# A pairwise outer product with batch normalization: long rows in descending order, stored in longer runs

## The chip, the cores and the metric

The kernel runs on one core of a Trainium2 chip. The time is that of one execution on the device, in microseconds (us); with one core it is that core's time. The profile is of one execution: its span runs from the first instruction to the last, and is a little shorter than the time of the execution.

## The reference

There are 1024 samples, 39 fields and 16 values a field. For each of the 741 pairs of fields (row r from 1 to 38, column c below r) the outer product of `xj[r]` and `xi[c]` is taken, normalized over all samples and its 256 entries, scaled and shifted by the pair's `gamma` and `beta`, and multiplied by `W`:

```python
_ROWS, _COLS = np.tril_indices(39, k=-1)          # 741 pairs, row by row
cross = xj[:, rows, :, None] * xi[:, cols, None, :]         # (1024, 741, 16, 16)
mean = jnp.mean(cross, axis=(0, 2, 3), keepdims=True)
var = jnp.mean(jnp.square(cross - mean), axis=(0, 2, 3), keepdims=True)
normed = (cross - mean) * jax.lax.rsqrt(var + 1e-5)
normed = normed * gamma[None, :, None, None] + beta[None, :, None, None]
out = normed[:, :, None, :, :] * W[None, None, :, :, :]
return jnp.transpose(out, (0, 2, 1, 3, 4))        # (1024, 1, 741, 16, 16) float32
```

The output is 777 MB; a pair of one sample is 256 values, 1 KB. In memory a sample's pairs lie one behind the other, row 1 first, so a row of r pairs is r KB without a gap, once for each sample.

## The kernel before

**Statistics.** Both inputs are loaded whole (6 MB). Each partition holds eight samples (`NT = 8`). Mean and variance of all pairs come from sums and a few small matrix products, without forming the pairs. From them `spread(group)` puts the scale and shift of some rows on all partitions (matrix products into PSUM), and `apply(group)` (L493 to L500, DVE) folds `gamma` and `beta` in and leaves the two coefficients of each pair in `st_sb`. `ROW_GROUPS` lists the groups: first row, last row plus one, PSUM bank, and the tile `n` behind which the group is applied. `SHORT_GROUP` names the group of rows 1 to 4.

**Tiles.** A tile is one row for two samples per partition (`T = 2`, 256 samples in all, so four tiles per row). The list `tiles` holds the row, the first of its two samples (`t0`), and its place in `y_sb`, counted in pairs. It begins with row 19 four times (tiles 0 to 3). Then come rows 20 to 38 in ascending order, each tile of a row r followed by a tile of its partner row 38 - r (row 38 has none). A row and its partner fill one half of `y_sb` (`half` = 76 pairs x 1 KB per partition), and the halves are used in turn. In its place a tile holds the r pairs of its first sample, then those of its second, and behind both stands the partner. Tiles 0 and 1 lie in the first half, 2 and 3 in the second; the statistics use the second half as scratch before.

**The steps of a tile.** The coefficients are folded in as follows:
- `scale_xi(n)` (L167, POOL) multiplies `xi` by the scale of each pair and leaves it in `xs` (two buffers).
- `products(n)` writes the outer products into `y_sb`: for each sample and each of the 16 values of `xj[r]` one instruction over all r pairs, some on ACT (L145), some on POOL (L147). POOL takes 4 of 16, or 5 for rows over 33 (`LONG`), or 6, 6, 5 for tiles 0 to 2. Rows 1 to 4 (`SHORT`) are done by DVE instead (L180, L190), from `xj_short`, a copy in PSUM that ACT makes once (L526).
- `finish(n)` adds the shift and multiplies by `W` in place. DVE does it by one L284 for a pair, both samples at once (tile 1, `RAW`, has one sample at a time). Some pairs are taken off DVE: POOL adds the shift (L270) and multiplies a few pairs together (L273); for rows over 33, ACT adds it (L268) and POOL multiplies, eight pairs in two steps of four.
- `store(n, c0, c1, t_from, t_to)` (L209) puts the pairs c0 to c1 out as DMAs of SP's queue. `bounds(n)` cuts a tile into pieces: by hand for the first eight (`FIRST_PIECES`), then one piece up to row `ONE`, two above. A store goes out when its piece is finished. The last piece of a row over `ONE` is one DMA for each sample; every other piece is one DMA for both.

Tile 0 takes another path (`affine` and `weigh`), which starts from raw products made during the statistics.

**Order.** The order on each engine is that of the program (`manual_schedule`), and engines wait for each other where data or places overlap. The loop over n issues `scale_xi(n + 2)`, `finish(n)`, `apply` of the groups due, and `products(n + 1)`. So on ACT the L268 of a tile stand ahead of the products of the next, on POOL stand `xs`, the end of the tile, then the next products, and on SP all stores stand in the order of the tiles. Products of a tile may start when the stores of what lay in its place have landed.

Of the kernel before, what the change touches and what calls it, by code (L numbers as in the profile page):

```python
# [14 lines left out]
T = 2  # L15


ONE, LONG = 24, 33
FIRST_PIECES = (
    (0, 1, 3, 6, 10, 14, 19), (0, 4, 9, 14, 19), (0, 4, 11, 19), (0, 9, 19), (0, 10, 20), (0, 9, 18), (0, 10, 20), (0, 9, 18)  # L20
)


# [6 lines left out]


ROW_GROUPS = (
    (19, 20, 0, None), (20, 21, 1, None), (15, 19, 1, 2), (21, 25, 2, 4), (1, 15, 2, 8), (25, 32, 3, 16), (32, 39, 4, 24)
)
SHORT_GROUP = 4


@with_exitstack
def tile_pair_outer_batchnorm(
# [17 lines left out]
    NB, F, E = xi.shape  # L57
# [8 lines left out]
    mid = (F - 1) // 2  # L66
    tiles = [(mid, t0, t0 // T * half // 2) for t0 in range(0, NT, T)]
    slot = 0
    for r in range(mid + 1, F):
        for t0 in range(0, NT, T):  # L70
            tiles.append((r, t0, slot * half))
            if r < F - 1:
                tiles.append((F - 1 - r, t0, slot * half + T * r))
            slot ^= 1

    RAW = 1
# [58 lines left out]
    def view(n):  # L135
        r, _, u = tiles[n]
        return y_sb[:, u : u + T * r, :].rearrange("p (t n) e -> p t n e", t=T)
# [23 lines left out]
    def scale_xi(n):  # L161
        r, t0, _ = tiles[n]
        if r <= SHORT:
            return
        n0 = first[r]
        xs = scaled.tile([P, T, r, E], F32, tag="xs", name=f"xs_{r}_{t0}")
        nc.gpsimd.tensor_tensor(  # L167
            xs,
            xi_sb[:, t0 : t0 + T, 0:r, :],
            s_sb[:, :, n0 : n0 + r, :].to_broadcast([P, T, r, E]),  # L170
            ALU.mult,
        )
        xs_of[n] = xs

    def products(n):

        r, t0, _ = tiles[n]
        if r <= SHORT:
            xs = scaled_short.tile([P, T, r, E], F32, tag="xs_short", name=f"xs_{r}_{t0}")
            nc.vector.tensor_tensor(  # L180
                xs,
                xi_sb[:, t0 : t0 + T, 0:r, :],
                s_short[:, first[r] : first[r] + r]
                .unsqueeze(1)
                .unsqueeze(3)
                .to_broadcast([P, T, r, E]),
                ALU.mult,
            )
            for t in range(T):
                nc.vector.tensor_tensor(  # L190
                    view(n)[:, t].rearrange("p n (i j) -> p n i j", j=E),
                    xs[:, t].unsqueeze(2).to_broadcast([P, r, E, E]),
                    xj_short[:, t0 + t, r - 1 : r, :].unsqueeze(3).to_broadcast([P, r, E, E]),
                    ALU.mult,
                )
            return
        xs = xs_of.pop(n)
        split = E - (POOL_I_FIRST[n] if n < 3 else POOL_I_LONG if tiles[n][0] > LONG else POOL_I)
        for t in range(T):
            for i in range(E):  # L200
                product(n, nc.scalar if i < split else nc.gpsimd, t, i, xs[:, t])

    def store(n, c0, c1, t_from=0, t_to=T):
        r, t0, _ = tiles[n]
        n0 = first[r]

        step = 1 if r > ONE and c1 == r else t_to - t_from
        for t in range(t_from, t_to, step):
            nc.sync.dma_start(  # L209
                out_v[:, t0 + t : t0 + t + step, (n0 + c0) * EE : (n0 + c1) * EE],  # L210
                view(n)[:, t : t + step, c0:c1, :].rearrange("p t n e -> p t (n e)"),
            )
# [14 lines left out]
    def weigh(n):  # L227

        y = view(n)
        for c0, c1 in zip(bounds(n), bounds(n)[1:]):  # L230
            affine(n, range(c0, min(c1, OWN)), (nc.vector,))
            nc.vector.tensor_tensor(  # L232
                y[:, :, c0:c1, :],
                y[:, :, c0:c1, :],
                w_dve.unsqueeze(1).to_broadcast([P, T, c1 - c0, EE]),
                ALU.mult,
            )
            store(n, c0, c1)

    def bounds(n):  # L240
        if n < len(FIRST_PIECES):
            return FIRST_PIECES[n]
        r = tiles[n][0]
        pieces = 1 + (r > ONE)
        return tuple(q * r // pieces for q in range(pieces + 1))

    def finish(n):


        r = tiles[n][0]  # L250
        n0 = first[r]
        y = view(n)
        long = r > LONG
        p1 = r // 2 if long else r
        if long:
            share = POOL_PAIRS_LONG
        elif RAW < n < 10:
            share = POOL_PAIRS_FIRST
        else:
            share = int(r * POOL_SHARE + 0.5) if r > SHORT else 0  # L260
        p0 = p1 - share
        step = POOL_PAIRS_LONG // 2 if long else r
        for c0 in range(p0, p1, step):
            c1 = min(c0 + step, p1)
            for c in range(c0, c1):
                t_c = t_sb[:, n0 + c : n0 + c + 1]
                if long:
                    nc.scalar.activation(y[:, :, c, :], y[:, :, c, :], AF.Identity, bias=t_c)  # L268
                else:
                    nc.gpsimd.tensor_scalar(  # L270
                        y[:, :, c, :], y[:, :, c, :], t_c, 1.0, ALU.add, ALU.mult
                    )
            nc.gpsimd.tensor_tensor(  # L273
                y[:, :, c0:c1, :],
                y[:, :, c0:c1, :],
                w_sb.unsqueeze(1).to_broadcast([P, T, c1 - c0, EE]),
                ALU.mult,
            )

        size = 1 if n == RAW else T  # L280
        for t in range(0, T, size):
            for c0, c1 in zip(bounds(n), bounds(n)[1:]):
                for c in [*range(c0, min(c1, p0)), *range(max(c0, p1), c1)]:
                    stt(  # L284
                        y[:, t : t + size, c, :],
                        y[:, t : t + size, c, :],
                        t_sb[:, n0 + c : n0 + c + 1],
                        w_dve.to_broadcast([P, size, EE]),
                        ALU.add,
                        ALU.mult,  # L290
                    )
                store(n, c0, c1, t, t + size)

    with tc.manual_schedule():
# [180 lines left out]
        def spread(group):  # L475
            r0, r1, bank, _ = ROW_GROUPS[group]
            n0, n1 = first[r0], first[r1 - 1] + r1 - 1
            at = used[bank]
            used[bank] = at + 2 * (n1 - n0)
            ps = ps_st[bank][:, at : used[bank]].rearrange("p (x n) -> p x n", x=2)  # L480
            for r in range(r0, r1):
                nc.tensor.matmul(  # L482
                    ps[:, :, first[r] - n0 : first[r] - n0 + r],
                    pick[:, r, :],
                    stq[:, :, 0:r],
                    start=True,
                    stop=True,
                )
            spread_of.append((ps, n0, n1))

        def apply(group):
            ps, n0, n1 = spread_of[group]
            nc.vector.tensor_mul(ps[:, 1], ps[:, 1], st_sb[:, 0, n0:n1])  # L493
            if group == SHORT_GROUP:

                nc.vector.tensor_mul(ps[:, 0], ps[:, 0], st_sb[:, 0, n0:n1])
                nc.vector.tensor_copy(st_sb[:, 0, n0:n1], ps[:, 0])
            else:
                nc.vector.tensor_mul(st_sb[:, 0, n0:n1], ps[:, 0], st_sb[:, 0, n0:n1])
            nc.vector.tensor_add(st_sb[:, 1, n0:n1], ps[:, 1], st_sb[:, 1, n0:n1])  # L500
# [8 lines left out]
        for group in range(1, len(ROW_GROUPS)):  # L509
            spread(group)  # L510
        s_short = spread_of[SHORT_GROUP][0][:, 0]
        apply(1)
        products(1)
        scale_xi(2)

        for n in range(1, len(tiles)):
            if n + 2 < len(tiles):
                scale_xi(n + 2)
            finish(n)
            for group, (_, _, _, tile_of) in enumerate(ROW_GROUPS):  # L520
                if n == tile_of:
                    apply(group)
            if n + 1 < len(tiles):
                products(n + 1)
            if n == 32:
                nc.scalar.copy(xj_short, xj_sb[:, :, 1 : SHORT + 1, :])  # L526


# [26 lines left out]
```

## Time and profile before

| what | value |
|---|---|
| median of six runs | 1881.4 us (1880.85 to 1882.86) |
| the profiled execution | 1881.56 us, span 1879.8 us |
| DVE busy | 1720.5 us, 92% of the span |
| ACT busy | 1642.9 us, 87% |
| POOL busy | 1532.1 us, 82% |
| written to memory | 776.99 MB, 417 GB/s over the span |
| DMA packets | 63994 |
| first store issued | 36.03 us |
| last store issued | 1861.92 us |

Busy time of an engine counts its instructions alone. A DMA packet is one run that one of the 16 DMA engines moves; 128 partitions are spread over them, eight to an engine. Of the packets, 4784 have under 512 bytes, most of them the writes of 4 bytes by which a DMA tells that it has landed. The rest of the profile is shown where it is used.

### The profile page before, as it was taken

How to read it: one execution, taken by the hardware profiler on the slowest of the kernel's cores; microseconds unless marked ns; L12 is line 12 of the kernel's file. 1: busy time of each engine (PE TensorE's matmuls, PEld its weight loads, DVE VectorE, ACT ScalarE, POOL GpSimd, SP SyncE). 2: the span in 40 equal slices, each digit the busy share in tenths (PEclk: the TensorE clock that was granted, in tenths of full speed). 3: DMA queues.
4: the chain of work that ended last, by engine and by line, in shares of the span. 5: the costliest groups of instructions: out<-in, count | busy, mean ns of one | idle time of the engine just before them, and what ended most of it. 6: DMA issues, size and time to landing. Idle time of an engine off the chain costs nothing. (4 is left out here: it accounts for less than half of the span.)

```text
span 1879.8 us, 9660 instructions
## 1 busy us (share of the span) xinstructions
PE 26.0 (1%) x130; PEld 23.3 (1%) x130; DVE 1720.5 (92%) x2625; ACT 1642.9 (87%) x3416; POOL 1532.1 (82%) x1746
## 2 busy tenths in 40 slices
PE   4000000000000000000000000000000000000000
PEld 4000000000000000000000000000000000000000
DVE  8999999998989898989898989898999999988885
ACT  7998989898989798989898989898988888888883
POOL 8999888888888788888888878787888777777873
DMA  5999999999999999999999999999999999999999
GB/s 198 386 421 426 430 426 430 426 426 425 425 427 424 424 424 426 424 426 424 424 424 426 424 426 423 417 425 422 423 419 426 423 424 422 424 419 415 426 414 411
DMA packets 63994, 783.63 MB, mean 417 GB/s; under 512 B 4784, under 2 KB 6448, under 8 KB 17072
## 3 DMA queue, kind: packets, MB, share of 16 engines
q1 hardware_dynamic: 62624, 779.72, 98.3%
q10 hardware_dynamic: 1296, 3.29, 0.5%
q14 instruction: 73, 0.60, 0.1%
q8 instruction: 1, 0.02, 0.0%
HBM read 6.00 MB, written 776.99 MB: 417 GB/s over the span
## 5 line engine op out<-in xcount | busy, mean ns | idle before, releaser
L284 DVE SCALAR_TENSOR_TENSOR y_sb<-y_sb,st_sb,w_dve 128x512 f32<-128x512 f32 (+1 forms) x2511 | 1651.0, 737 | 132.2 <-issue 119.6
L145 ACT ACTIVATE y_sb<-xs,xj_sb 128x288 f32<-128x288 f32 (+20 forms) x3194 | 1510.8, 566 | 192.8 <-DMA out_dram<-y_sb 165.2
L147 POOL TENSOR_SCALAR y_sb<-xs,xj_sb 128x416 f32<-128x416 f32 (+29 forms) x1126 | 604.8, 561 | 40.9 <-DMA out_dram<-y_sb 27.7
L273 POOL TENSOR_TENSOR y_sb<-y_sb,w_sb 128x2048 f32<-128x2048 f32 (+3 forms) x155 | 517.3, 3343 | 104.0 <-ACT y_sb L268 94.5
L167 POOL TENSOR_TENSOR xs<-xi_sb,st_sb 128x640 f32<-128x640 f32 (+33 forms) x135 | 184.0, 1363 | 171.2 <-ACT y_sb L145 164.9
L270 POOL TENSOR_SCALAR y_sb<-y_sb,st_sb 128x512 f32<-128x512 f32 x291 | 196.8, 692 | 0.1
L268 ACT ACTIVATE y_sb<-y_sb,st_sb 128x512 f32<-128x512 f32 x160 | 100.2, 708 | 1.9
L190 DVE TENSOR_TENSOR y_sb<-xs,ps 128x1024 f32<-128x1024 f32 (+3 forms) x32 | 24.8, 817 | 0.6
L482 PE MATMUL ps<-y_sb 39*128 39x38 f32 (+37 forms) x76 | 16.5, 398 | 2.8 <-DVE y_sb L468 2.8
L482 PEld LDWEIGHTS ps<-y_sb 39*128 39x128 f32 x76 | 16.3, 329 | 3.1 <-DVE y_sb L468 3.1
L346 ACT ACTIVATE y_sb<-y_sb 128x1248 f32<-128x1248 f32 x8 | 9.9, 1244 | 2.8 <-POOL y_sb L335 2.7
L351 DVE TENSOR_REDUCE y_sb<-y_sb 128x78 f32<-128x1248 f32 x8 | 11.2, 1446 | 0.3 <-ACT y_sb L346 0.3
L145 ACT ACTIVATE y_sb<-xi_sb,xj_sb 128x304 f32<-128x304 f32 x24 | 11.4, 537 | 0.0
L335 POOL TENSOR_TENSOR y_sb<-xi_sb,y_sb 128x1248 f32<-128x1248 f32 x4 | 9.2, 2319 | 2.4 <-ACT y_sb L384 2.4
L232 DVE TENSOR_TENSOR y_sb<-y_sb,w_dve 128x2048 f32<-128x2048 f32 (+4 forms) x6 | 10.7, 1838 | 0.1
L325 DVE TENSOR_REDUCE y_sb<-xi_sb 128x39 f32<-128x624 f32 (+1 forms) x6 | 6.1, 1012 | 3.8 <-DMA xi_sb<-in_r_xi_dram 3.8
L335 POOL TENSOR_TENSOR y_sb<-xj_sb,y_sb 128x1248 f32<-128x1248 f32 x4 | 9.2, 2316 | 0.0
L371 PE MATMUL ps<-y_sb 128*39 128x79 f32 x48 | 8.1, 340 | 15.6 <-DVE y_sb L351 15.4
L225 POOL TENSOR_SCALAR y_sb<-y_sb,st_sb 128x512 f32<-128x512 f32 x8 | 6.4, 812 | 2.1 <-ACT y_sb L145 2.1
L325 DVE TENSOR_REDUCE y_sb<-xj_sb 128x39 f32<-128x624 f32 (+1 forms) x6 | 6.1, 1016 | 1.2 <-DMA xj_sb<-in_r_xj_dram 1.2
L223 ACT ACTIVATE y_sb<-y_sb,st_sb 128x512 f32<-128x512 f32 x9 | 6.5, 800 | 0.2 <-ACT y_sb L145 0.2
L371 PEld LDWEIGHTS ps<-y_sb 128*39 128x39 f32 x48 | 5.9, 178 | 17.6 <-DVE y_sb L351 10.4
(59 smaller groups left out, 35.1 us busy)
## 6 DMA issues: line engine op xcount, KB each, us to landing
out_dram<-y_sb SPq DMA_DIRECT2D x25, 2304.0 KB, 14.7
out_dram<-y_sb SPq DMA_DIRECT2D x12, 4352.0 KB, 15.4
out_dram<-y_sb SPq DMA_DIRECT2D x12, 4096.0 KB, 16.3
out_dram<-y_sb SPq DMA_DIRECT2D x10, 4608.0 KB, 14.7
out_dram<-y_sb SPq DMA_DIRECT2D x12, 3840.0 KB, 17.5
out_dram<-y_sb SPq DMA_DIRECT2D x21, 2048.0 KB, 17.0
out_dram<-y_sb SPq DMA_DIRECT2D x12, 3584.0 KB, 18.1
out_dram<-y_sb SPq DMA_DIRECT2D x12, 3328.0 KB, 18.1
```

Source lines behind the costliest of these rows:

```text
L145: nc.scalar.activation(y, src, AF.Copy, scale=scale)
L147: engine.tensor_scalar(y, src, scale, 1.0, ALU.mult, ALU.mult)
L167: nc.gpsimd.tensor_tensor(xs, xi_sb[:, t0 : t0 + T, 0:r, :], s_sb[:, :, n0 : n0 + r, :].to_broadcast([P, T, r, E]), ALU.mult,)
L190: nc.vector.tensor_tensor(view(n)[:, t].rearrange("p n (i j) -> p n i j", j=E), xs[:, t].unsqueeze(2).to_broadcast([P, r, E, E]), xj_short ...
L268: nc.scalar.activation(y[:, :, c, :], y[:, :, c, :], AF.Identity, bias=t_c)
L270: nc.gpsimd.tensor_scalar(y[:, :, c, :], y[:, :, c, :], t_c, 1.0, ALU.add, ALU.mult)
L273: nc.gpsimd.tensor_tensor(y[:, :, c0:c1, :], y[:, :, c0:c1, :], w_sb.unsqueeze(1).to_broadcast([P, T, c1 - c0, EE]), ALU.mult,)
L284: stt(y[:, t : t + size, c, :], y[:, t : t + size, c, :], t_sb[:, n0 + c : n0 + c + 1], w_dve.to_broadcast([P, size, EE]), ALU.add, ALU.mult,)
L325: nc.vector.tensor_reduce(total[:, t0:t1, part(x)], sources[x][:, t0:t1], AX.X, ALU.add)
L335: nc.gpsimd.tensor_tensor(devs[n % 7], sources[x][:, t0 : t0 + T], shift[:, x : x + 1, :].unsqueeze(3).to_broadcast([P, T, F, E]), ALU.sub ...
L371: nc.tensor.matmul(ps_g[acc][0:F, 0 : 2 * F + 1], lhs, fb[:, t], start=t == 0, stop=t == NT - 1)
L482: nc.tensor.matmul(ps[:, :, first[r] - n0 : first[r] - n0 + r], pick[:, r, :], stq[:, :, 0:r], start=True, stop=True,)
```

## The change

It has four parts. The rows over 19 come in descending order, 38 first; row 38 so fills the places of tiles 0 to 3, and row 20 comes last. `ONE` goes from 24 to 30, so rows 25 to 30 are one piece. From tile 6 on, `store` writes rows over 19 one sample at a time: the first sample in its pieces, the second sample whole, at the last piece. The first two tiles of row 38 (4 and 5) are cut into four pieces by hand, of which the last is one DMA for each sample. The groups of rows, the tile at which `xj_short` is copied and the tiles with `POOL_PAIRS_FIRST` follow the new order; the coefficients of the second group are applied in the loop at n = 1 and not ahead of `products(1)`.

```diff
-ONE, LONG = 24, 33
+ONE, LONG = 30, 33
 FIRST_PIECES = (
-    (0, 1, 3, 6, 10, 14, 19), (0, 4, 9, 14, 19), (0, 4, 11, 19), (0, 9, 19), (0, 10, 20), (0, 9, 18), (0, 10, 20), (0, 9, 18)
+    (0, 1, 3, 6, 10, 14, 19), (0, 4, 9, 14, 19), (0, 4, 11, 19), (0, 9, 19), (0, 10, 19, 29, 38), (0, 10, 19, 29, 38)
 )
 ROW_GROUPS = (
-    (19, 20, 0, None), (20, 21, 1, None), (15, 19, 1, 2), (21, 25, 2, 4), (1, 15, 2, 8), (25, 32, 3, 16), (32, 39, 4, 24)
+    (19, 20, 0, None), (38, 39, 1, 1), (34, 38, 1, 4), (1, 5, 1, 5), (29, 34, 2, 28), (5, 10, 2, 29),
+    (25, 29, 3, 68), (10, 14, 3, 69), (20, 25, 4, 100), (14, 19, 4, 101),
 )
-SHORT_GROUP = 4
+SHORT_GROUP = 3
...
-    for r in range(mid + 1, F):
+    for r in range(F - 1, mid, -1):
         for t0 in range(0, NT, T):
             tiles.append((r, t0, slot * half))
...
-        step = 1 if r > ONE and c1 == r else t_to - t_from
+        whole = n >= len(FIRST_PIECES)
+        step = 1 if r > mid and (whole or c1 == r) else t_to - t_from
         for t in range(t_from, t_to, step):
+            if whole and step == 1 and t == t_to - 1:
+                if c1 < r:
+                    continue
+                c0 = 0
             nc.sync.dma_start(
...
-        elif RAW < n < 10:
+        elif RAW < n < 4:
             share = POOL_PAIRS_FIRST
...
-        apply(1)
         products(1)
         scale_xi(2)
...
-            if n == 32:
+            if n == 5:
                 nc.scalar.copy(xj_short, xj_sb[:, :, 1 : SHORT + 1, :])
```

## The prediction

> **What bounds the kernel now.** I read the page's slices first, then the DMA view over long stretches, then the time line of single engines, and the chain of waits last.
>
> ```profile
> DVE  8999999998989898989898989898999999988885
> ACT  7998989898989798989898989898988888888883
> DMA  5999999999999999999999999999999999999999
> GB/s 198 386 421 426 430 426 430 426 426 425 425 427 424 424 424 426 424 426 424 424 424 426 424 426 423 417 425 422 423 419 426 423 424 422 424 419 415 426 414 411
> ...
> q1 hardware_dynamic: 62624, 779.72, 98.3%
> ```
>
> From the third slice on the 16 DMA engines are busy throughout; no compute engine is. The end is set by 777 MB going out. So only three things count: when the first store starts, what a byte costs, and the holes in which DMA has nothing to send. A store in flight hides every engine's work.
>
> What a packet costs comes from the DMA view of two stretches with one form of store each (rows 20 to 23, one run per sample; rows 25 to 30, two runs):
>
> ```profile
> DMA packets 5444, 100.02 MB, mean 427 GB/s; under 512 B 320, under 2 KB 320, under 8 KB 320
> ...
> DMA packets 19769, 237.79 MB, mean 425 GB/s; under 512 B 1516, under 2 KB 1516, under 8 KB 1772
> ```
>
> The first is 200 to 434 us, the second 600 to 1160 us. Packets under 512 B are 4-byte semaphore writes, so 5124 and 18253 carry data. Sixteen engines give 16 x 234 = 3744 = 5124a + 100.02b and 16 x 560 = 8960 = 18253a + 237.79b; hence a = 0.0097 us per packet and b = 36.94 engine-us per MB. Put into 83 to 1862 us (754.02 MB, 53286 data packets) this needs 28368 / 16 = 1773.0 of 1779 us: **6.0 us of holes**. 1390 to 1860 us (rows 34 to 38; 197.90 MB, 14496 packets) holds 4.3 of them.
>
> ```profile
> 424.76 7.43 ACT L145 ACTIVATE y_sb<-xs,xj_sb 128x240 f32<-128x240 f32 x19
> 434.45 6.17 ACT L145 ACTIVATE y_sb<-xs,xj_sb 128x384 f32<-128x384 f32 x12 [2.27 <-DMA out_dram<-y_sb]
> 443.64 21.18 ACT L145 ACTIVATE y_sb<-xs,xj_sb 128x384 f32<-128x384 f32 x48 [3.01 <-DMA out_dram<-y_sb]
> ```
>
> This is one of their sources: row 23 gives way to row 24, which takes two pairs more than row 23 had, so its second sample overlaps the place of row 23's partner and waits for that later store too (3.01 us); DMA runs dry at 464 us.
>
> The other place to look is the start, where POOL has no idle time:
>
> ```profile
> 60.02 1.28 POOL L167 TENSOR_TENSOR xs<-xi_sb,st_sb 128x640 f32<-128x640 f32 x1
> 61.28 2.02 POOL L270 TENSOR_SCALAR y_sb<-y_sb,st_sb 128x512 f32<-128x512 f32 x3
> 63.38 3.44 POOL L273 TENSOR_TENSOR y_sb<-y_sb,w_sb 128x1536 f32<-128x1536 f32 x1
> 66.80 3.97 POOL L147 TENSOR_SCALAR y_sb<-xs,xj_sb 128x304 f32<-128x304 f32 x8
> 72.01 1.17 POOL L167 TENSOR_TENSOR xs<-xi_sb,st_sb 128x576 f32<-128x576 f32 x1 [1.24 <-DVE st_sb L500]
> 73.15 2.03 POOL L270 TENSOR_SCALAR y_sb<-y_sb,st_sb 128x512 f32<-128x512 f32 x3
> 75.26 3.45 POOL L273 TENSOR_TENSOR y_sb<-y_sb,w_sb 128x1536 f32<-128x1536 f32 x1
> 78.67 4.10 POOL L147 TENSOR_SCALAR y_sb<-xs,xj_sb 128x320 f32<-128x320 f32 x8
> 82.85 1.28 POOL L167 TENSOR_TENSOR xs<-xi_sb,st_sb 128x640 f32<-128x640 f32 x1
> ```
>
> L284 of tile 4 started at 82.80 us, when POOL's products ended; its first store went out at 89.62, and DMA stayed fed with no more than a microsecond to spare.
>
> **The change, part by part.** Times are set against the profiled execution: span 1879.8, whole 1881.56, which is 0.16 above the median of six, 1881.4.
>
> *Fewer packets.* Per partition and tile, rows 25 to 30 go from 4 runs to 2: 6 rows x 4 tiles x 2 = 48. Rows 31 to 37 go from 4 to 3: 28. Row 38 goes from 16 over its four tiles to 8 + 8 + 3 + 3 = 22: minus 6. The four tiles 20, 18, 20, 18 lose their halves: 8. In all 78 x 128 = 9984 packets, x 0.0097 / 16 = **6.05 us less**. The number of DMAs changes by a handful, one more for rows 20 to 24 and one fewer for rows 25 to 30; an issue on SP takes 0.4 to 1.25 us of a queue that waits for DVE most of the time (1436 us in its waits). Runs of 25 to 38 KB don't occur in this trace (the longest packet is 24 KB), so their price is an extrapolation: at worst nothing is saved; a fit over 6 us stretches of the packets gives 10.0 ns, 6.2 us. I take 6.05.
>
> By the Trainium skill ("DMA: Bandwidth & Descriptors", "Why small descriptors are slow (HBM only)") a packet carries about 3 cycles of overhead, and joining descriptors pays only at 256 B or less; that speaks against this part. At the 850 MHz that the page gives I estimate 3.5 ns, or 2.2 us saved, and the whole sum would end at +2.2 us instead of -1.65. The two stretches above decide, at 9.7 ns.
>
> *The start.* Tile 4 is now row 38 instead of row 20, and fills the places of tiles 0 and 1. Its `xs` needs the coefficients of row 38, whose L493 to L500 now follow L284 of tile 1 instead of preceding it. L284 can start at some 47.0 us instead of 47.49; 34 instructions of the 256-wide row take 13.4, the three coefficient steps 0.55: POOL's `xs` starts at 60.95. From there POOL is back to back: `xs` of 38 pairs 2.28 (row L167, 1216 wide), end of tile 2 5.52 (L270 and L273 above), products of tile 3 3.97, hence 72.7; `xs` 2.28, end of tile 3 5.52, ten 608-wide products 7.5 (0.75 each): **88.0**. ACT is done before that (22 x 0.70 = 15.4 from 69.97). DVE finishes tile 3 at 72.7 + 10.7 = 83.4 and waits 4.7 us.
>
> What DMA sees: an issue into an empty queue moves data after 0.95 us (68.16 to 69.05, 63.67 to 64.63). It ran dry at 78.5 in the profile of before and restarted at 79.0; tile 3's first store now goes at 78.85 and starts at 79.8, 0.8 more of a hole. Its two pieces take 5.6 + 6.2 us, to 91.6. The first piece of tile 4 follows ten L284, at 88.1 + 6.7 = 94.8, moving at 95.8: a hole of 4.2. Tiles 4 and 5 then go out in four pieces each, in time, 23.6 us a tile (one sample of one partition is 38 KB in four packets, 38 x 0.0378 + 4 x 0.0097 = 1.475 us; an engine has 8 partitions of two samples, 16 x 1.475), to 143.0. Tile 6 takes tile 4's place: first sample landed 117.0, ACT 15.4 to 132.4, the `xj_short` copy 0.6 (row L526), four L268 2.7, two L273 9.0: half of the first sample goes at 144.7, moves at 145.7, hole 2.7. It is one sample's half, 5.8 us, to 151.5; all else waits for 30 L284 (19.84, as at 1794.16 us), 152.3 + 0.95: hole 1.7. Tile 7, by the same steps, 0.5. **Sum +9.9 us.** Bounds: 5.0 if only the holes before 96 us are real; 14.3 if tile 7 loses as much as tile 6. I take the rows' sum.
>
> *Descending order.* A shorter row lies inside its predecessor's place and waits for no partner; storing sample by sample also frees the first sample before the second. The 6.0 us of holes should go. Check on later rows, from D, the landing of the second sample two long tiles ago: row 37 needs 0.4 + 11 x 0.685 + 29 x 0.66 = 27.1, +0.95 = 28.0 to its last stores, while the queue lasts 23.3 + 0.6 + 5.5 = 29.4. Row 30, stored only when whole: 0.4 + 7.1 + 17.2 + 0.95 = 25.7 against 4.9 + 18.3 + 4.9 = 28.1. Both keep over a microsecond. Bounds: none recovered, 0; all, 6.0. I take **5.5 us less**.
>
> *At nothing.* The regrouped coefficients (three DVE steps of 0.2 to 0.4 us a group) are hidden by stores in flight; uncovered, the three groups more would cost some 2 us in all. `RAW < n < 4` moves a pair between POOL and DVE in a few tiles, hidden likewise. The last tile's stores drain at full rate (428 GB/s in 1862 to 1878 us) whichever row is last.
>
> Sum: -6.05 + 9.9 - 5.5 = **-1.65**, so about 1878.1 for the span and **1879.7** on the median.
>
> **Rivals.**
> - *The start costs half.* If tile 6 finds its place free sooner, or the queue is fuller, the holes after 140 us (4.9) vanish: 1874.8. For it: they rest on margins of 2 to 3 us. Against it: ACT needs 15.4 us per tile and cannot start earlier.
> - *The early store is too small (slower).* Half of one sample covers 5.5 us, but in rows 36 to 38 the step from mid store to last store took 6.8 to 8.2 us (1640.19 to 1647.00, 1805.83 to 1814.03). Where a mid store comes as the queue runs dry, DMA idles 6.8 + 0.95 - 5.5 = 2.2 us. On the four tiles of row 37: +8.8, 1888.5. It decides from three tiles on (6.6 against 5.5 up to 1885.2). Against it: the margin of 1.4 us above; a late tile also frees its partner's place early.
> - *It doesn't do what it says:* runs over 24 KB are cut into packets again; no saving: 1879.7 + 6.05 = 1885.8. Nothing in the trace shows such a cut.
>
> **How the numbers follow.** Within 0.2% (3.8 us, about what a measurement of this kernel can tell from no change) is 1877.6 to 1885.2. Forecast 0.55, its own range 1876.5 to 1883; its lower edge, 0.14, counts as faster, 0.41 as same. Half the start 0.24, faster. Early store too small 0.16 and cut runs 0.05, slower. Faster 0.38, same 0.41, slower 0.21. The range leaves out a tenth at each end: down to 1873.5 for the first rival, up to 1887.5, short of the second at its full price.
>
> **What would show it.** Some 9984 fewer packets on queue 1, and over 426 GB/s in rows 25 to 30. In the first 160 us: DVE idle before L284 near 84 to 88 us, and 5 us windows with a DMA share well under 1 near 92 and 144 to 153 us. After 200 us no window under 0.95. The prediction is wrong if DMA runs dry in rows 31 to 37, if packets stay as many, or if the start shows no hole.

## The result, and the profile after

The changed kernel is slower: 1886.19 us in the median of 15 runs (1885.89 to 1887.39) against 1881.38 us (33 runs, 1880.66 to 1882.86). The ratio is 1.0026, with a 95% interval of 1.0019 to 1.0033. The forecast was 1879.7. Of the runs below, one execution in four of the kernel with 4200 added matrix products took 5642.66 us instead of 1921.4, and is left out.

The profiled execution took 1887.39 us, with a span of 1885.7. These are the slices and queues of its page that answer to those of before:

```profile
DVE  7898889999999999999999999999999999999994
ACT  7989888888889998888999999998999888888882
...
DMA  4899999999999999999999999999999999999998
GB/s 189 362 401 384 427 423 430 423 430 423 430 422 428 423 426 427 425 426 416 428 428 427 428 433 424 430 427 427 430 429 424 428 430 427 425 431 424 431 425 351
DMA packets 53946, 783.63 MB, mean 416 GB/s; under 512 B 4720, under 2 KB 6384, under 8 KB 17008
...
q1 hardware_dynamic: 52576, 779.72, 97.5%
...
q14 instruction: 73, 0.60, 0.1%
```

Three things differ. The first four slices (to 189 us) are lower, the third and fourth with 401 and 384 against 421 and 426 GB/s. The middle is higher. And the last slice has fallen from 411 to 351, where no hole was expected. The packets went as worked out: 10048 fewer on queue 1, of which 64 are semaphore writes, so 9984 of data.

Stretches of 5 us show both losses (columns: from and to, length; busy time of PE, weight loads, DVE, ACT, POOL with the number of instructions; then clock, DMA share, GB/s):

```profile
85.00:90.00 5.00, 0.00 (x0) 0.00 (x0) 1.06 (x2) 2.47 (x5) 4.92 (x7) 1.00 1.00 416
90.00:95.00 5.00, 0.00 (x0) 0.00 (x0) 5.00 (x9) 5.00 (x9) 4.68 (x2) 1.00 0.48 198
95.00:100.00 5.00, 0.00 (x0) 0.00 (x0) 5.00 (x8) 5.00 (x8) 5.00 (x2) 1.00 0.71 295
140.00:145.00 5.00, 0.00 (x0) 0.00 (x0) 5.00 (x8) 2.86 (x5) 5.00 (x2) 1.00 0.78 326
145.00:150.00 5.00, 0.00 (x0) 0.00 (x0) 5.00 (x9) 5.00 (x9) 5.00 (x6) 1.00 0.59 249
150.00:155.00 5.00, 0.00 (x0) 0.00 (x0) 4.32 (x7) 5.00 (x8) 3.92 (x6) 1.00 0.58 249
1870.00:1875.00 5.00, 0.00 (x0) 0.00 (x0) 0.00 (x0) 0.00 (x0) 0.00 (x0) 1.00 0.98 419
1875.00:1880.00 5.00, 0.00 (x0) 0.00 (x0) 0.00 (x0) 0.00 (x0) 0.00 (x0) 1.00 0.33 140
1880.00:1885.00 5.00, 0.00 (x0) 0.00 (x0) 0.00 (x0) 0.00 (x0) 0.00 (x0) 1.00 0.08 33
```

The holes at the start are there, at the places that were worked out. The last ten microseconds are the new thing: all stores have been issued by 1859.74 us, no engine computes, and yet most of the DMA engines have nothing left while a few still write. Before, every DMA engine finished within 0.2 us of the others.

How many engines those are can be read from the landings. A store raises its semaphore once for each of the 16 DMA engines, so a store's first and last increments tell how far apart the engines are. The five last increments of one store, in us behind the store's first:

```
store landing at about    500 us               1190 us                1760 us                1870 us
before            .16 .23 .49 1.57 1.79   .25 2.75 3.17 3.98 5.18  .11 .13 .15 .19 1.34   .11 .13 .15 .16 .19
after             .18 .19 .55 1.19 1.47   .16 1.30 2.82 3.38 3.61  .21 2.50 4.83 5.77 8.26  .26 2.84 4.79 6.44 8.78
```

Twelve engines run together and four are late, until the queue runs dry for the twelve and the late ones catch up. Before, that happened again and again up to row 38, and behind the last of these stretches all engines were together:

```profile
1215.00:1220.00 5.00, 0.00 (x0) 0.00 (x0) 5.00 (x9) 3.56 (x6) 4.83 (x10) 1.00 0.84 351
1735.00:1740.00 5.00, 0.00 (x0) 0.00 (x0) 5.00 (x9) 5.00 (x8) 5.00 (x7) 1.00 0.86 354
1830.00:1835.00 5.00, 0.00 (x0) 0.00 (x0) 5.00 (x9) 5.00 (x9) 5.00 (x7) 1.00 0.76 323
```

In the changed kernel the worst makes up some 2 us around 870 us (the last increment is 3.5 us late at 846 us, 1.4 at 885). After that nothing stops the late engines, and the worst ends 8.6 us late.

### The profile page after: what moved, and what is told of

The parts are those of the page before. It is cut to its first block, busy times and chain, and to the rows that moved or that the text cites. A ratio compares the mean times of both kernels' runs of the same rounds, so it can differ in the third digit from the quotient of the medians.

```text
span 1885.7 us, 9636 instructions
## 1 busy us (share of the span) xinstructions
PE 26.0 (1%) x130; PEld 23.3 (1%) x130; DVE 1725.3 (91%) x2637; ACT 1645.8 (87%) x3416; POOL 1527.0 (81%) x1743
## 4 chain that ended last, share of the span: by engine, by line
DMA 39%; ACT 14%; DVE 8%; issue 1%; SPq 0%; POOL 0%; ACTq 0%; DVEq 0%; POOLq 0%
DMA out_dram<-y_sb 39%; ACT y_sb L147 14%; DVE y_sb L291 8%; SPq L216 0%; POOL y_sb L277 0%; ACTq L147 0%; DVEq L556 0%; DVEq L291 0%; POOLq L277 0%
## 5 line engine op out<-in xcount | busy, mean ns | idle before, releaser
L147 ACT ACTIVATE y_sb<-xs,xj_sb 128x512 f32<-128x512 f32 (+21 forms) x3194 | 1514.8, 565 | 188.3 <-DMA out_dram<-y_sb 151.9
L149 POOL TENSOR_SCALAR y_sb<-xs,xj_sb 128x464 f32<-128x464 f32 (+27 forms) x1126 | 604.6, 560 | 11.7 <-DMA out_dram<-y_sb 9.2
L169 POOL TENSOR_TENSOR xs<-xi_sb,st_sb 128x1216 f32<-128x1216 f32 (+33 forms) x135 | 183.9, 1363 | 215.0 <-ACT y_sb L147 204.9
L192 DVE TENSOR_TENSOR y_sb<-xs,ps 128x256 f32<-128x256 f32 (+3 forms) x32 | 24.8, 817 | 0.6
## 6 DMA issues: line engine op xcount, KB each, us to landing
out_dram<-y_sb SPq DMA_DIRECT2D x23, 2304.0 KB, 10.3
```

The source lines that it names most:

```text
L147: nc.scalar.activation(y, src, AF.Copy, scale=scale)
L149: engine.tensor_scalar(y, src, scale, 1.0, ALU.mult, ALU.mult)
L169: nc.gpsimd.tensor_tensor(xs, xi_sb[:, t0 : t0 + T, 0:r, :], s_sb[:, :, n0 : n0 + r, :].to_broadcast([P, T, r, E]), ALU.mult,)
L192: nc.vector.tensor_tensor(view(n)[:, t].rearrange("p n (i j) -> p n i j", j=E), xs[:, t].unsqueeze(2).to_broadcast([P, r, E, E]), xj_short ...
```

## The experiments

All medians are in us; ratios are to the kernel before, run beside them on the same chip (1881.52 for the first four, 1881.34 for the last three; beside the changed kernel it was 1881.38, so medians of different sets can be compared to some 0.2).

**Row 20 first.** The row loop of the changed kernel, with the tables that follow from it:

```diff
-    for r in range(F - 1, mid, -1):
+    for r in [mid + 1, *range(F - 1, mid + 1, -1)]:
...
 # FIRST_PIECES, apply(1) and RAW < n < 10 as before; ROW_GROUPS and SHORT_GROUP refitted
```

> The changed kernel, but with row 20 (and its partner 18) still standing behind the row 19 tiles, cut as before; then 38 down to 21, stored as changed. Theory S (the DMA engine that is behind all others sets the end; later holes and the ragged end are the same loss of the other engines, seen at two places): the 9.4 us of holes at 92 to 155 us go, nothing else: 1886.2 - 9.4 = 1876.8, the last DMA still lands over 8 us. Rival M (the mean of the 16 engines counts; the ragged end is a loss of its own): the same time. Rival O (descending order or storing by sample costs time in itself): over 1881.

Measured 1879.36, ratio 0.9989 (0.9980 to 0.9998), which is 2.6 us over S and M and clearly under O. Starting with row 38 had cost 6.8 us. Most of the difference to 9.4 is seen in the trace: row 38 now comes at tile 12 and still opens smaller holes (1.7 us in all, near 139, 192 and 240 us). The last store's increments lay 8.2 us apart.

**The old order with the new stores.** The kernel before, with `ONE = 30` and the changed `store`:

```diff
-ONE, LONG = 24, 33
+ONE, LONG = 30, 33
...
-        step = 1 if r > ONE and c1 == r else t_to - t_from
+        whole = n >= len(FIRST_PIECES)
+        step = 1 if r > mid and (whole or c1 == r) else t_to - t_from
...
```

> The kernel before in its ascending order and with its first eight tiles, but rows 25 to 30 in one piece and samples stored one by one as changed. S: only the packets go, about 9984 x 0.0097 / 16 = 6 us off the engine that is behind: 1875. M: the same 6 us, holes of 6 us stay, end not ragged: 1875. Rival O (whole rows are stored too late for an order in which each new row waits for its predecessor's partner): new holes eat the gain, 1880 or more.

Measured 1918.75, ratio 1.0198 (1.0184 to 1.0212). Both S and M missed this; O is right in its direction, though not in size. The stretches around one change of row in this run:

```profile
1030.00:1035.00 5.00, 0.00 (x0) 0.00 (x0) 5.00 (x9) 4.48 (x8) 4.83 (x12) 1.00 0.94 393
1035.00:1040.00 5.00, 0.00 (x0) 0.00 (x0) 5.00 (x9) 5.00 (x10) 5.00 (x7) 1.00 0.24 100
1040.00:1045.00 5.00, 0.00 (x0) 0.00 (x0) 3.53 (x7) 5.00 (x11) 1.49 (x4) 1.00 0.93 393
...
1021.50 21.82 DVE L289 SCALAR_TENSOR_TENSOR y_sb<-y_sb,st_sb,w_dve 128x512 f32<-128x512 f32 x33 [9.05 <-issue]
1030.52 14.75 ACT L145 ACTIVATE y_sb<-xs,xj_sb 128x480 f32<-128x480 f32 x26 [2.10 <-DMA out_dram<-y_sb]
```

The last two lines are of the time line (start, duration, engine and line, idle time before and what ended it): DVE had stood idle for 9.05 us, and ACT waited 2.10 us for a store to land, just ahead of the hole. DMA ran dry like this at some 95 us intervals (941, 1039, 1138, 1235 us and so on), one change of row apart. So the old order does not carry the new stores. The likely reason, read from the order of the places and these waits, is that a longer row waits for its predecessor's partner and then delivers nothing until it is whole.

**The new order with the old stores.** The reverse: the changed kernel, `ONE = 24` and the old `step`.

```diff
-ONE, LONG = 30, 33
+ONE, LONG = 24, 33
...
-        whole = n >= len(FIRST_PIECES)
-        step = 1 if r > mid and (whole or c1 == r) else t_to - t_from
+        step = 1 if r > ONE and c1 == r else t_to - t_from
```

> The changed kernel with the stores of before (two pieces from row 25 on, both samples in one DMA but for the last piece), in the new order. S and M: the packets come back, 6 to 7 us: 1892 to 1893.5. If the longer runs saved nothing: 1886. If the stores by sample are what makes the start's holes: below 1886.

Measured 1889.50, ratio 1.0043 (1.0030 to 1.0056). The new stores are worth 3.3 us in this order, half of what either theory gave. The hole at 153 us is missing here (it belongs to the small early store of tile 6, some 2 us), so without that hole the packets would be worth some 5 us.

**Row 38 last.** As the first run, with row 38 behind all others (`ROW_GROUPS` refitted):

```diff
-    for r in [mid + 1, *range(F - 1, mid + 1, -1)]:
+    for r in [mid + 1, *range(F - 2, mid + 1, -1), F - 1]:
```

> As the run with row 20 first, but row 38 stands at the very end: 20, 37 down to 21, 38. S: its tiles make the DMA queue run dry near the end and let the engine that is behind catch up; that costs and brings nothing, the time is within 1.5 us of the run with row 20 first (1876.8), the last DMA lands within 2 us instead of over 8. M: the ragged end, 7 us of the mean engine, goes and 2.4 us of holes come: 4 to 5 us below that run, about 1872.

Measured 1876.97 (10 runs, 1876.88 to 1877.41), ratio 0.9976 (0.9967 to 0.9986): **0.24% under the kernel before**, and under the changed one too. The run it is compared with took 2.4 us more, between the two expectations. Its stretches near the end:

```profile
1770.00:1775.00 5.00, 0.00 (x0) 0.00 (x0) 5.00 (x9) 5.00 (x8) 5.00 (x2) 1.00 0.54 230
1775.00:1780.00 5.00, 0.00 (x0) 0.00 (x0) 5.00 (x8) 3.31 (x5) 5.00 (x5) 1.00 0.53 224
1780.00:1785.00 5.00, 0.00 (x0) 0.00 (x0) 5.00 (x9) 4.03 (x6) 4.76 (x7) 1.00 0.75 319
1785.00:1790.00 5.00, 0.00 (x0) 0.00 (x0) 1.64 (x3) 4.91 (x8) 1.16 (x1) 1.00 0.81 342
...
1865.00:1870.00 5.00, 0.00 (x0) 0.00 (x0) 0.00 (x0) 0.00 (x0) 0.00 (x0) 1.00 1.01 436
```

About 6.9 us of the mean engine are lost in these 20 us (5 x 0.46, 0.47, 0.25 and 0.19), more than in any such stretch of the kernel before once its stores run (from 85 us on), and it is the fastest kernel of all. A count over the engine furthest behind says why. It can be kept for every store: that engine is dry from its last landing (less 0.35 us, from packet to semaphore) until the next store's issue plus 0.95 us. The account of each profiled execution:

```
                        first packet   last landing   dry to 85 us   dry later   the rest
before                       36.95        1878.76          3.68         0.00      1838.1
after                        38.05        1884.77          4.42         8.76      1833.5
row 20 first                 36.58        1876.58          3.89         1.73      1834.4
old order, new stores        36.82        1916.34          3.83        36.91      1838.8
new order, old stores        36.83        1886.65          4.51         6.79      1838.5
row 38 last                  37.08        1874.76          3.94         0.29      1833.4
row 38 last, old stores      36.65        1878.32          3.78         0.00      1837.9
```

The rest is what remains of the time from first packet to last landing: 1837.9 to 1838.5 in the three runs with the old stores, 1833.4 to 1834.4 in three of the four with the new ones. The old order with the new stores is the exception, 1838.8. Its dry time is a sum over 23 holes, so 0.2 us more for each would bring it into line, but that isn't shown. The run with row 38 last is ahead of the first because this engine was dry for 1.4 us less and had 0.9 less in the rest; the holes near 1775 us were in the other engines, which waited for it.

**Row 38 last with the old stores.** The edit to `store` and `ONE` is that of the run with the new order and the old stores.

> The kernel with row 38 at the end (1876.97 us), but with the stores of before: 10240 packets more and no hole at the start. S (only the DMA engine that is furthest behind counts; its work between the holes fell by 4.6 us from before to after): 1881.6 to 1882.5. By the mean of the engines, whose busy time fell by 7.3 us: 1884.3. If the stores by sample brought nothing beside the start's holes: 1877.

Measured 1881.20 (11 runs, 1880.88 to 1881.69), ratio 0.9999 (0.9990 to 1.0008). It is 4.2 us over the run before it, just under S's interval and well under the mean's. So the packets (10240 between these two runs) are worth 4.2 to 4.6 us, and the order by itself, with old stores and no row 38 at the start, is worth nothing within 2 us either way: the 6 us of holes of the kernel before were not won. By the two constants of the forecast the mean engine still loses 5.9 us after 200 us here, against 6.3 before. Holes went from the middle and came back behind 1700 us (4.6 us, against 2.9), where row 38 now lets the late engine catch up.

**Why four engines fall behind.** Queue 14 fetches instructions, and that was the first theory. Over the whole run 73 packets of 8192 B at 0.309 us are 23 us; were they spread over 16 engines, they would be 1.4 us each. From 155 us on 68 of them make 21.0 us, and the four late engines' delays at the end, 8.58 + 6.30 + 4.59 + 2.75, add up to 22.2. The three largest stand to each other like the instructions on the page, ACT 3416, DVE 2637, POOL 1743 (1 : 0.73 : 0.53 against 1 : 0.77 : 0.51). To test it, instructions were added to TensorE, idle from 50 us on:

```diff
             spread(group)
+        for _ in range(4200):
+            nc.tensor.matmul(ps_s[:, 0:128], w_sb[:, 0, 0:128], w_sb[:, 0, 0:128], start=True, stop=True)
```

> The changed kernel plus 4200 small matrix products on TensorE, which is idle and has no other work by then; nobody reads or waits for them. Theory F (a DMA engine falls behind because it also fetches an engine's instructions, in packets of 8192 B and 0.309 us on queue 14): some 8400 instructions more are 66 packets, 20 us, on one DMA engine, nearly all behind the start's holes. If that engine fetches for TensorE alone it ends up 20 us behind instead of 8.6 for the worst: 1886 + 11 = 1897; if it is the worst one already, 1905. Rival H (some DMA engines are slower by nature or carry more data): 1886, last DMA lands over 8.6 us as without.

The control has an eighth of them, with `range(525)` and 512 columns of `xj_sb` as the moving operand.

> The control: an eighth of the instructions, 525 matrix products, each four times as wide, so TensorE is busy for long but hardly fetches (1050 instructions, 8 packets, 2.5 us). F: less than the worst engine is behind already, 1886 within 1. If TensorE's activity in itself slows the kernel: above 1888.

Measured 1921.38 with the many, ratio 1.0211 (1.0196 to 1.0227), and 1890.65 with the few, ratio 1.0048 (1.0034 to 1.0062). From the page of the run with many and then of that with few (share of TensorE, queues):

```profile
PE 966.5 (50%) x8530; PEld 963.8 (50%) x8530; DVE 1725.7 (90%) x2637; ACT 1648.0 (86%) x3416; POOL 1532.1 (80%) x1743
...
q8 instruction: 66, 1.08, 0.2%
q14 instruction: 73, 0.60, 0.1%
```

```profile
PE 478.9 (25%) x1180; PEld 223.5 (12%) x1180; DVE 1725.6 (91%) x2637; ACT 1646.1 (87%) x3416; POOL 1530.2 (81%) x1743
...
q14 instruction: 73, 0.60, 0.1%
q8 instruction: 9, 0.15, 0.0%
```

Both expectations of F missed their numbers, and the control came out above 1888. Each product is two matrix instructions and two weight loads here (8530 and 8530 on the page, 130 and 130 without), twice what was expected. TensorE fetches on queue 8, in packets of 16 KB, 65 and 8 more than without. The cost follows these packets, or the number of instructions, which goes with them: 35.2 us for 65 is 0.54 each, 4.5 us for 8 is 0.56 each; 16 KB of a store come to 0.61 by the two constants of the forecast. It does not follow TensorE's busy time, which only doubles from one to the other, and DVE, ACT and POOL are as busy as without it. While TensorE ran, DMA carried 410 GB/s against 426 without (200 to 980 us), and afterwards 428 as without. In the control a store's last increment stands 0.20 us behind its first at 245 us and 2.36 us at 250 us, with a packet of queue 8 at 250.66 us. So a fetch packet delays a DMA engine, and the stores with it. But the engine furthest behind does not take up that cost: it ends 10.3 us late with the many and 9.8 with the few, against 8.6.

Nor is that engine late because of queue 14. Increments of single stores of the changed kernel, on both sides of a packet of queue 14 (the four last, in us behind the store's first):

```
first increment at   four last               packet of queue 14 at
1743.0 us            2.52 4.03 5.86 8.22
1749.4 us            2.50 4.83 5.77 8.26     1747.6 us
1766.3 us            2.51 4.59 5.77 8.37
1772.7 us            2.49 4.52 6.57 8.40     1773.6 us
1789.2 us            2.55 4.36 6.39 8.55
1795.4 us            3.31 4.28 6.29 8.58     1794.8 us
```

Each of these packets makes one of three engines some 0.8 us later, more than the 0.309 us that it takes, and that engine works it off over the next stores. The fourth, which sets the end, is passed over. From 1232 to 1842 us the last increment goes from 3.7 to 8.9 us late while 27 packets of queue 14 come. Apart from two steps of 0.6 us, it rises by at most 0.21 us from one store to the next. The run with row 20 first does the same (3.4 to 8.5 us), and so does the one with few products (4.9 to 10.1). So F is seen at work on the other three engines, but H stands for the one that sets the end, and the agreement of 21.0 with 22.2 us proves nothing. What holds that engine back is open: writing alone at the very end, it takes 0.686 us for a packet of 18432 B, where 0.691 is the median of all of that size, so its packets are not slower. The trace doesn't say which of the 16 engines it is.

## Why the prediction was wrong

**Fewer packets: right in number, a quarter too much in worth.** 9984 went. The price held for runs up to 38 KB: with the two constants found before, the changed kernel's 600 to 1160 us (238.86 MB, 13636 data packets) come to 559.7 of 560 us. The rule of 3 cycles that the prediction cites, by which 2.2 us would be saved, gives too little. But on the engine that counts the rest fell by 4.6 us (1838.1 to 1833.5), and 4.2 us by the medians, not 6.05; the times of queue 1's packets, summed and divided by 16, fell by 9.4 (the expectation of the run with row 38 last and the old stores took 7.3; with 9.4 it would say 1886.4, still further off). Why the engine that is behind gains less is open.

**The start: right.** From the time line of POOL and DVE (start, duration, engine and line):

```profile
61.80 2.27 POOL L169 TENSOR_TENSOR xs<-xi_sb,st_sb 128x1216 f32<-128x1216 f32 x1 [0.77 <-DVE st_sb L507]
...
81.41 7.49 POOL L149 TENSOR_SCALAR y_sb<-xs,xj_sb 128x608 f32<-128x608 f32 x10
...
88.94 19.84 DVE L291 SCALAR_TENSOR_TENSOR y_sb<-y_sb,st_sb,w_dve 128x512 f32<-128x512 f32 x30 [4.73 <-POOL y_sb L149]
```

DVE waited 4.73 us for POOL's products (4.7 worked out) and started at 88.94; 88.1 was forecast, and in this execution the first store stood 1.1 us later than before. By the two constants, the holes of the mean engine were 9.7 us more (9.2 from 85 to 200 us and 0.5 before, without the later first store), where 9.9 was forecast; the engine that is behind was dry for 9.5 us more (8.76 + 0.74). The rival that halves the start is refuted: the two holes after 140 us are 5.0 us. (The upper bound of 14.3 should be 13.8: it counts tile 7's 0.5 twice.)

**Descending order: the step that failed.** It was put as "The 6.0 us of holes should go ... I take 5.5 us less". They did go: by the two constants the mean engine lost 6.3 us after 200 us before, and 0.3 after, up to the first increment of the last store. But they were worth nothing. The constants describe the mean of 16 engines, and a DMA share under 1 was read as lost time, when it was most of the engines waiting for one that still had work. That engine was never dry after 85 us in the kernel before. The same mistake stands in "The last tile's stores drain at full rate (428 GB/s in 1862 to 1878 us) whichever row is last": that was so before because row 38 came last and let all engines meet. Now 7.4 us of the mean engine come back as a ragged end, from the last store's first increment to its last.

With the right engine the sum closes: -4.6 for packets and +9.5 for the start are +4.9; the medians give +4.8. In the profiled execution the later first packet adds 1.1. Of the 6.5 us between forecast and measurement, 5.5 are this step and 1.5 the packets; the start takes off 0.4.

**The rivals.** The early store of one sample was too small only in tile 6, at 153 us, where the forecast itself had a hole of 1.7; from row 37 on no such hole came. Runs over 24 KB are not cut: 256 packets have 38912 B. Of the signs that were named, fewer packets, 427 GB/s in 600 to 1160 us, DVE idle at 84 to 88 us and low windows near 92 and 144 to 153 us came. "After 200 us no window under 0.95" did not: dozens of 5 us windows show 0.85 to 0.94 (0.85 at 865 to 870 us), though the engine that is behind was dry in none of them, and the last ten microseconds show 0.33 and 0.08.

## What to carry to other kernels

When stores bound a kernel, keep the account for the DMA engine that is furthest behind, and not for the mean share: compare a store's first and last landing, and take a hole for lost only if that engine is dry too. Big tiles cost most at the start of such a pipeline, when nothing is queued: row 38 there made 9.5 us of dry time, at the end 0.3. Order and size of stores belong together: descending rows gained nothing with the old stores (1881.2), the new stores cost 37 us in the old order (1918.8), and the two together gained 4.4 us once the largest row stood last (1877.0).

## What the runs showed of the hardware

Instruction fetch is DMA traffic, and a packet of it falls on a single DMA engine: 8 KB of queue 14 made one engine's landings some 0.8 us later than the others'. Apart from that, one of the 16 engines fell behind steadily, by 5.1 us in 609 us of stores, and that sets the end when nothing lets it catch up. The Trainium skill ("Runtime: NRT & Kernel Launch", "Instruction fetch mechanics") has each engine stream its instructions by a DMA queue of its own, in blocks of 16 KiB, with the cost mostly hidden. Only two queues carry instructions in these traces. The packets of queue 8, which grew with TensorE's instructions, agree in size (16 KB); those of queue 14 are 8 KB; and in a kernel whose stores hardly pause the cost was not hidden, at 0.54 to 0.56 us for each 16 KB.
